# Scores and exp of the last two context blocks by halves of the queries, and other PSUM buffers and another order in the linear attention

## The chip, the cores and the metric

The kernel runs on one core of a Trainium2 chip. The metric is the device time of one execution in microseconds. The engines are TensorE (PE, matmuls; PEld, its weight loads), VectorE (DVE), ScalarE (ACT), GpSimd (POOL) and SyncE (SP, which issues the DMAs). Each works through its own instructions in order.

## What is computed

The reference is one block of a perceiver network: a cross attention of 512 queries on 8192 context tokens, a linear attention on the 512 tokens, and a feed-forward layer with quantized operands. Width is 512, with 16 heads of 32.

```python
x = x + xattn(layernorm(x), ctx, ctx, Wq, bq, Wk, bk, Wv, bv, Wo, bo)
#   q, k, v = split_heads(...); weights = softmax(q k^T / sqrt(32)); z = weights v; z Wo + bo
x = x + attn(layernorm(x), w_qkv, proj, w_out, b_out)
#   qf = elu(q proj) + 1; kf = elu(k proj) + 1       (128 features a head)
#   out = qf (kf^T v) / (qf sum(kf) + 1e-8);          out w_out + b_out
x = x + ffn(layernorm(x), W1, b1, W2, b2)
#   linear layers on operands rounded to 8 bits, gelu between them
```

## The kernel before

`network` does all of it, in stages that follow each other; a second copy of it stands under a condition at the program's end and is run only where denominators leave a range, which they do not here. Almost every instruction is passed through `in_order`, so that each engine's order is the order of the source.

**Cross attention.** The context comes in 16 blocks `b` of 512 tokens. For a block, keys `kT[b]` and values `vt[b]` are projected; for all but the last block by `blockwise` (seven products of quarter size, matmuls of 256 columns, `pm`), in the last block the keys by `project_keys` (matmuls of 512 columns, `pk`). These steps stand in a list, `queue`, and are dealt out by `ahead`, each with a cost, so that they come due evenly over the units.

A unit is (b, g, k): a block, one of 4 groups of 4 heads, and one of 4 chunks of 128 keys. The loop is `for i, u in enumerate(units)`. For a unit:

- `weights` (L788, L797): TensorE forms the scores `sc` of 128 keys, 4 heads and 512 queries, in eight matmuls of 32 rows and 64 columns, eight at a time on the array. `sc` is in PSUM, four stretches of 512 columns, one for each head. Its pool `ps_s` has one buffer. ScalarE takes exp of all of `sc` in one instruction into `ex` (four buffers).
- Then TensorE does the due projection steps (L388) and, in `weighted_sums` (L733), the product `av` of the unit before, into the pool `ps_a` of two buffers.
- `summed` (L806): VectorE adds `ex` to `acc`, from which the denominators come (`sums`, `dn`, L751; `inverse`, a reciprocal, L757).

In the last block's units `weighted_sums` stands before the due step, and `dn` is formed in between.

**Linear attention.** For each of four groups `g`: `keys(g)` and `queries(g)` project (L1007) and VectorE copies the result out of PSUM (L1012); `key_features` and `query_features` multiply with `proj` into `feat` (L1051, L1073; the pool `ps_f`, one buffer); `elu1` takes exp and relu of two halves on ScalarE (`er`, L1029) and joins them on VectorE (`f`, L1033). Between the two halves of `f` on VectorE stands what `between` does, one of the projections with its copy. `products` gives `kv` (L1085, L1091) and copies it, `turned` transposes it (`kvl`, L1101, L1103), `attended` forms the numerator and the denominator `att` (L1112) and copies the denominator (`de`, L1117), `divided` takes its reciprocal and multiplies (L1122, L1123). `out_sums` (L898) is the output projection `po`, and `out_added` (L1174, L1178) adds it to `xs` and forms statistics for the next layer norm.

PSUM here: `ps_m` (tag `pt`, two buffers), `ps_a` (tag `av`, two), `ps_f` (the size of four). After the last `feat`, `ps_f` is closed and `ps_o` (four buffers) takes its place.

**Feed-forward.** Two quantized layers with bf16 matmuls; some matmuls (`nothing`, `keep_busy`) give no result that is used and only keep TensorE occupied.

The functions that the change touches, and what calls them:

Of the kernel before, what the change touches and what calls it, by code (L numbers as in the profile page):

```python
# [8 lines left out]
F32 = mybir.dt.float32  # L9
BF16 = mybir.dt.bfloat16  # L10
AF = mybir.ActivationFunctionType
# [5 lines left out]
P = 128  # L17
# [9 lines left out]
def network(  # L27
# [24 lines left out]
    nc = tc.nc  # L52
    S, E = x.shape
    L = ctxT.shape[1]
    FF = W1T.shape[1]
    H, D = 16, 32
# [3 lines left out]
    HG = P // D  # L60
# [3 lines left out]
    SCALE = 1.0 / float(D) ** 0.5  # L64
# [12 lines left out]
    def in_order(i):  # L77

        return tc.keep_in_program_order(i)
# [6 lines left out]
    for i in range(7):  # L86
        n = 1 << i
# [190 lines left out]
    ap4 = ctx.enter_context(tc.tile_pool(name="ap4", bufs=4))  # L278
    ps_m = ctx.enter_context(tc.tile_pool(name="ps_m", bufs=2, space=PSUM))

    with ExitStack() as actx:
        aw = actx.enter_context(tc.tile_pool(name="aw", bufs=1))

        qT = aw.tile([P, NE, S], F32, name="qT")
# [11 lines left out]
        bias = aw.tile([P, NE], F32, name="bias")  # L296
# [4 lines left out]
        ct, kT, vt, tt = {}, {}, {}, {}  # L301
# [4 lines left out]
        total = first + NB  # L306
# [416 lines left out]
        ps_a = ctx.enter_context(tc.tile_pool(name="ps_a", bufs=2, space=PSUM))  # L723
        sctx = actx.enter_context(ExitStack())
        ps_s = sctx.enter_context(tc.tile_pool(name="ps_s", bufs=1, space=PSUM))
        av, late = {}, []
# [35 lines left out]
        def biased(g):  # L762
# [5 lines left out]
            else:  # L768
                in_order(nc.vector.tensor_scalar(
                    Z[:, g, :], Z[:, g, :], bv_sb[:, g : g + 1], None, ALU.add  # L770
                ))

        def weights(b, g, k):

            assert ("k", b, g, k // 2) in made
            sc = ps_s.tile([P, HG, S], F32, name="sc")
            if exact:
                for j in range(HG):
                    for h in range(2):
                        in_order(nc.tensor.matmul(  # L780
                            sc[ts(h, P // 2), j, :], lhsT=ones_h[ds(j * D, 3), ts(h, P // 2)],
                            rhs=mrow[ds(j * D, 3), g, :], start=True, stop=False,
                        ))

            for j in range(HG):
                rows = ts(j, D)
                for h in range(2):
                    in_order(nc.tensor.matmul(  # L788
                        sc[ts(h, P // 2), j, :],
                        lhsT=kT[b][rows, g, ds(k * P + h * P // 2, P // 2)],  # L790
                        rhs=qT[rows, g, :], start=not exact, stop=True,
                    ))
            ex = ap4.tile([P, HG, S], F32, name="ex")
            if exact:
                in_order(nc.scalar.activation(ex, sc, AF.Exp, scale=SCALE))
            else:
                in_order(nc.scalar.activation(  # L797
                    ex, sc, AF.Exp, bias=bias[:, g : g + 1], scale=SCALE
                ))
            return ex  # L800
# [36 lines left out]
        for i, u in enumerate(units):  # L837
            ex = weights(*u)
            if i >= last_block:
                b, g, k = u  # L840
# [48 lines left out]
        ps_o = octx.enter_context(tc.tile_pool(name="ps_o", bufs=NT, space=PSUM))  # L889
# [97 lines left out]
    with ExitStack() as lctx:  # L987
        lw = lctx.enter_context(tc.tile_pool(name="lw", bufs=1))
        lp = lctx.enter_context(tc.tile_pool(name="lp", bufs=2))
# [9 lines left out]
        eps_c = lw.tile([P, 1], F32, name="eps_c")  # L999
        nc.vector.memset(eps_c, 1e-8)  # L1000

        kT2, qT2, kf, kf_sum, qf, kvT, kvl = {}, {}, {}, {}, {}, {}, {}

        def projected(wt, g, name):
            ps = ps_m.tile([P, S], F32, name="pq2", tag="pt")
            for c in range(NE):
                in_order(nc.tensor.matmul(  # L1007
                    ps, lhsT=wt[:, c, ts(g, P)], rhs=ynT[:, c, :],
                    start=(c == 0), stop=(c == NE - 1),
                ))  # L1010
            dst = lp.tile([P, S], F32, name=name)
            in_order(nc.vector.tensor_copy(dst, ps))  # L1012
            return dst

        def keys(g):
            kT2[g] = projected(wk2_sb, g, "kT2")

        def queries(g):
            qT2[g] = projected(wq2_sb, g, "qT2")

        def elu1(ps, halves, between):


            f = ap4.tile([P, HG, S], F32, name="f", tag="ex")
            er = []
            for h in halves:
                er.append(ap2.tile([P, 2, HG // 2, S], F32, name="er", tag="vt"))
                for d, function in enumerate((AF.Exp, AF.Relu)):
                    in_order(nc.scalar.activation(  # L1029
                        er[-1][:, d].rearrange("p a n -> p (a n)"), ps[h], function  # L1030
                    ))
            for i, h in enumerate(halves):
                in_order(nc.vector.scalar_tensor_tensor(  # L1033
                    f[h], er[i][:, 0].rearrange("p a n -> p (a n)"), 1.0,
                    er[i][:, 1].rearrange("p a n -> p (a n)"), ALU.min, ALU.add,
                ))
                if i == 0:
                    between()
            return f

        by_head = [(slice(None), ts(i, HG // 2)) for i in range(2)]
        by_token = [(slice(None), slice(None), ts(i, S // 2)) for i in range(2)]
# [21 lines left out]
                kf_sum[g], half[:, :, :F], half[:, :, F:], ALU.add  # L1064
            ))

        def query_features(g, between):

            ps = ps_f.tile([P, HG, S], F32, name="feat")
            for j in range(HG):  # L1070
                rows = ts(j, D)
                for h in range(2):
                    in_order(nc.tensor.matmul(  # L1073
                        ps[ts(h, P // 2), j, :], lhsT=proj_sb[rows, g, ts(h, P // 2)],
                        rhs=qT2[g][rows, :], start=True, stop=True,
                    ))
            qf[g] = elu1(ps, by_token, between)

        def products(g):


            ps = ps_m.tile([P, 2, F], F32, name="kv", tag="pt")
            for t in range(NT):
                for j in range(HG):
                    in_order(nc.tensor.matmul(  # L1085
                        ps[ts(j, D), 0, :], lhsT=va[:, t, ds(g * P + j * D, D)],
                        rhs=kf[g][:, j, ts(t, F)],
                        start=(t == 0), stop=(t == NT - 1),
                    ))
            for j in range(HG):  # L1090
                in_order(nc.tensor.matmul(  # L1091
                    ps[ts(j, D), 1, :], lhsT=ones_c, rhs=kf_sum[g][:, j, :],
                    start=True, stop=True,
                ))
            kvT[g] = lp.tile([P, 2, F], F32, name="kvT")
            in_order(nc.scalar.copy(kvT[g], ps))

        def turned(g, copy=nc.scalar.copy):
            ps = ps_m.tile([P, 2, P], F32, name="kvl", tag="pt")
            for i in range(2):  # L1100
                in_order(nc.tensor.transpose(ps[:, i, :], kvT[g][:, i, :], ident))  # L1101
            kvl[g] = lp.tile([P, 2, P], F32, name="kvl")
            in_order(copy(kvl[g], ps))  # L1103

        def attended(g, n, pools):

            ps = []
            for i in range(2):
                pool, tag = pools
                ps.append(pool.tile([P, S], F32, name="att", tag=tag)[:, : n.size])  # L1110
                for j in range(HG):
                    in_order(nc.tensor.matmul(  # L1112
                        ps[i][ts(j, D), :], lhsT=kvl[g][:, i, ts(j, D)],
                        rhs=qf[g][:, j, n], start=True, stop=True,
                    ))
            de = lp.tile([P, S], F32, name="de")[:, : n.size]
            in_order(nc.scalar.activation(de, ps[1], AF.Identity, bias=eps_c))  # L1117
            return ps[0], de

        def divided(g, n, att):  # L1120
# [18 lines left out]
        key_features(1, lambda: queries(0))  # L1139
        products(0)  # L1140
        query_features(0, lambda: keys(2))
        turned(0), products(1)
        key_features(2, lambda: queries(1))
        turned(1)
        divided(0, every, attended(0, every, (ps_a, "av")))
        query_features(1, lambda: keys(3))
        products(2)
        key_features(3, lambda: queries(2))
        turned(2)
        divided(1, every, attended(1, every, (ps_a, "av")))  # L1150
        query_features(2, lambda: queries(3))
        products(3)


        po = [ps_m.tile([P, E], F32, name="po", tag="pt")]
# [5 lines left out]
        att = attended(2, every, (ps_a, "av"))  # L1161
# [2 lines left out]
        query_features(3, lambda: None)  # L1164

        po += [ps_m.tile([P, E], F32, name="po", tag="pt")]
        fctx.close()
        ps_o = ctx.enter_context(tc.tile_pool(name="ps_o", bufs=NT, space=PSUM))
        po += [ps_o.tile([P, E], F32, name="po2", tag="po") for _ in range(2)]

        def out_added(t):

# [8 lines left out]

        out_sums(1, [0, 1]), out_sums(2, [0, 1])
        halves = [ts(i, S // 2) for i in range(2)]
        att = attended(3, halves[0], (ps_a, "av"))
        divided(3, halves[0], att)
        out_sums(3, [0])
        att = attended(3, halves[1], (ps_o, "po"))
# [123 lines left out]
    for q in range(NF // 4):  # L1311
# [14 lines left out]
        for i in range(4):  # L1326
# [8 lines left out]
            if f < 2 or i % 2 == 1:  # L1335
                k = f if f < 2 else f // 2 + 1
# [33 lines left out]
    for i in range(len(chunks) + 1):  # L1370
        if i < len(chunks):
            f, n = chunks[i]
# [4 lines left out]
        f, n = chunks[i - 1]  # L1377
# [77 lines left out]
```

## Time and profile before

| | us |
|---|---|
| runs | 1117.04, 1117.11, 1119.11 (median 1117.11) |
| profiled execution | 1118.67, of which the span of its trace is 1116.9 |
| TensorE busy in the span | 1089.1 (98%) |
| VectorE, ScalarE, GpSimd busy | 932.2, 633.7, 177.8 |
| units of the block before the last begin | at 848.7 |
| units of the last block begin | at 902.2 |
| first output projection of the cross attention | at 957.6 |
| last matmul of the linear attention's output projection ends | at about 1059 |
| granted TensorE clock, mean | 0.995 |

A row of the profile's groups or of its timeline names the line of the kernel, the engine, the operation and the tiles (output <- inputs). In the timeline the first two columns are the start and the length in us; in square brackets stands how long the engine had been idle and which instruction ended the wait. A matmul of fp32 operands is done in two passes and shows as two records, so eight matmuls read x16. Ends of matmuls are modelled. A list of waits has: who waited <- for whom, us in total, times, the longest.

### The profile page before, as it was taken

Reading aid. Unit: us, or ns where it says so; the run is one execution under the profiler, and the core shown is the slowest. Engines: PE = TensorE matmul, PEld = TensorE weight load, DVE = VectorE, ACT = ScalarE, POOL = GpSimd, SP = SyncE. Lnnn points to the kernel's source line nnn. Section 1 sums busy time; section 2 is a strip of 40 time slices with the busy share of each in tenths; the row PEclk is TensorE's granted clock in tenths of the full one; section 3 lists DMA queues with packets and bytes.
Section 4 is the critical chain, followed back from the end, with each engine's and each line's share of the span. In section 5 each row is a group of like instructions: output and inputs, shape, how many; then the busy total and the mean of one; then the engine's idle time right before and its main releaser. Section 6 shows DMA issues by size and latency. Waiting matters only on the chain.

```text
span 1116.9 us, 31051 instructions
## 1 busy us (share of the span) xinstructions
PE 1089.1 (98%) x14331; PEld 409.7 (37%) x14336; DVE 932.2 (83%) x863; ACT 633.7 (57%) x425; POOL 177.8 (16%) x90
## 2 busy tenths in 40 slices
PE   8999999999999999999999999999999999999896
PEld 5433333333333333333333333333332321344342
DVE  3688999999888888888888888888888888756796
ACT  2155555566666666666665555555555566346253
POOL 3520303011403030403030303030300000023000
PEclk9999999999999999999999999999999999999999
DMA  7121213110302121212010101010110021130001
GB/s 264 38 79 40 96 40 96 58 59 30 95 31 68 50 76 30 75 51 68 30 58 2 40 2 40 2 39 2 40 39 2 2 77 39 38 151 2 1 1 41
DMA packets 24778, 55.56 MB, mean 50 GB/s; under 512 B 1984, under 2 KB 2496, under 8 KB 24384
## 3 DMA queue, kind: packets, MB, share of 16 engines
q1 hardware_dynamic: 24352, 52.97, 14.3%
q8 instruction: 114, 1.87, 0.7%
q10 hardware_dynamic: 288, 0.52, 0.1%
q14 instruction: 24, 0.20, 0.1%
HBM read 48.25 MB, written 5.24 MB: 48 GB/s over the span
## 4 chain that ended last, share of the span: by engine, by line
PE 88%; ACT 5%; DVE 5%; issue 1%; DMA 1%; SPq 0%; DVEq 0%; ACTq 0%
PE pm L388 35%; PE sc L788 24%; PE av L733 18%; ACT ex L797 4%; PE po L898 2%; PE pq L1007 2%; PE pq L136 1%; DVE unchanged L143 1%; PE pv L936 1%; PE pys L1356 1%; DVE de L1122 1%; ACT er L1029 1%; PE att L1112 1%; DMA ct<-in_ctxT 1%; DVE tops L631 0%
## 5 line engine op out<-in xcount | busy, mean ns | idle before, releaser
L797 ACT ACTIVATE ex<-sc,bias 128x2048 f32<-128x2048 f32 x256 | 504.3, 1970 | 358.4 <-PE sc L788 358.4
L806 DVE TENSOR_TENSOR acc<-acc,ex 128x2048 f32<-128x2048 f32 x248 | 584.8, 2358 | 73.2 <-ACT ex L797 72.9
L788 PE MATMUL sc<-qT,kT 32*64 32x512 f32 x4096 | 285.2, 613 | 6.9 <-ACT ex L797 6.7
L733 PE MATMUL av<-ex,vt 128*32 128x512 f32 x2048 | 266.9, 593 | 0.0
L383 POOL TENSOR_TENSOR tt<-ct 128x512 f32<-128x512 f32 x32 | 62.4, 1950 | 573.4 <-DMA ct<-in_ctxT 519.8
L788 PEld LDWEIGHTS sc<-qT,kT 32*64 32x64 f32 x4096 | 59.7, 129 | 221.8 <-ACT ex L797 198.0
L388 PE MATMUL pm<-w,tt 128*32 128x256 f32 x2048 | 127.0, 382 | 0.0
L388 PE MATMUL pm<-tt,w 128*32 128x256 f32 x1920 | 118.0, 382 | 0.0
L388 PE MATMUL pm<-w,ct 128*32 128x256 f32 x1536 | 96.5, 383 | 0.0
L478 DVE TENSOR_TENSOR vt<-vt,pm 128x512 f32<-128x512 f32 x112 | 75.3, 684 | 25.1 <-PE pm L388 24.1
L388 PEld LDWEIGHTS pm<-w,tt 128*32 128x32 f32 x2048 | 59.7, 109 | 86.0 <-issue 51.9
L388 PE MATMUL pm<-ct,w 128*32 128x256 f32 x1440 | 90.1, 383 | 1.2 <-DMA ct<-in_ctxT 1.2
L733 PEld LDWEIGHTS av<-ex,vt 128*32 128x32 f32 x2048 | 65.3, 110 | 55.5 <-issue 14.0
L383 POOL TENSOR_TENSOR tt<-ct,tt 128x512 f32<-128x512 f32 x32 | 85.3, 2666 | 1.3
L388 PEld LDWEIGHTS pm<-tt,w 128*32 128x32 f32 x1920 | 56.5, 109 | 77.6 <-issue 46.2
L388 PEld LDWEIGHTS pm<-w,ct 128*32 128x32 f32 x1536 | 43.3, 109 | 73.8 <-issue 47.0
L388 PEld LDWEIGHTS pm<-ct,w 128*32 128x32 f32 x1440 | 41.2, 109 | 67.2 <-issue 44.1
L478 DVE TENSOR_TENSOR kT<-kT,pm 128x512 f32<-128x512 f32 x60 | 40.8, 680 | 27.6 <-PE pm L388 27.0
L481 DVE SCALAR_TENSOR_TENSOR kT<-pm,bk_sb,kT 128x256 f32<-128x256 f32 x90 | 39.0, 474 | 2.9 <-PE pm L388 1.0
L745 DVE TENSOR_TENSOR Z<-Z,av 128x512 f32<-128x512 f32 x60 | 40.6, 677 | 0.0
L1029 ACT ACTIVATE er<-feat 128x1024 f32<-128x1024 f32 x32 | 30.2, 1029 | 9.7 <-PE feat L1051 7.4
L1033 DVE SCALAR_TENSOR_TENSOR f<-er 128x1024 f32<-128x1024 f32 x16 | 19.9, 1248 | 13.6 <-ACT er L1029 13.6
(181 smaller groups left out, 585.7 us busy)
## 6 DMA issues: line engine op xcount, KB each, us to landing
ct<-in_ctxT SPq DMA_DIRECT2D x15, 1024.0 KB, 5.3
wraw<-in_W1T SPq DMA_DIRECT2D x16, 512.0 KB, 3.8
wraw<-in_W2T SPq DMA_DIRECT2D x16, 512.0 KB, 3.8
wd<-wquant SPq DMA_DIRECT2D x16, 256.0 KB, 2.4
w_q<-wd SPq DMA_DIRECT2D x2, 2048.0 KB, 10.6
w<-in_w_qkv SPq DMA_DIRECT2D x3, 1024.0 KB, 5.1
w<-in_Wk SPq DMA_DIRECT2D x2, 512.0 KB, 6.5
ct<-in_ctxT SPq DMA_DIRECT2D x2, 512.0 KB, 7.5
```

What stands on the lines that cost most here:

```text
L383: in_order(nc.gpsimd.tensor_tensor(tt[b][:, i], x, y, ALU.subtract))
L388: in_order(nc.tensor.matmul(ps[ts(j, D)], lhsT=lhsT[:, ts(j, D)], rhs=rhs, start=start, stop=stop))
L478: in_order(nc.vector.tensor_tensor(dst, src, ps, ALU.add))
L481: in_order(nc.vector.scalar_tensor_tensor(dst[:, m, :], ps[:, m, :], bk_sb[:, 2 * i + m : 2 * i + m + 1], src[:, m, :], ALU.add, ALU.add,))
L733: in_order(nc.tensor.matmul(av[g][ts(j, D), :], lhsT=vt[b][:, k, ds(g * P + j * D, D)], rhs=ex[:, j, :], start=(k == 0), stop=(k == NC - 1),))
L745: in_order(nc.vector.tensor_tensor(Z[:, g, :], Z[:, g, :], ps, ALU.add))
L788: in_order(nc.tensor.matmul(sc[ts(h, P // 2), j, :], lhsT=kT[b][rows, g, ds(k * P + h * P // 2, P // 2)], rhs=qT[rows, g, :], start=not ex ...
L797: in_order(nc.scalar.activation(ex, sc, AF.Exp, bias=bias[:, g : g + 1], scale=SCALE))
L806: in_order(nc.vector.tensor_tensor(acc[:, g], acc[:, g], ex, ALU.add))
L898: in_order(nc.tensor.matmul(po, lhsT=lhsT[:, c, ts(t, P)], rhs=w[:, c, :], start=(c == 0), stop=(c == NE - 1),))
L1007: in_order(nc.tensor.matmul(ps, lhsT=wt[:, c, ts(g, P)], rhs=ynT[:, c, :], start=(c == 0), stop=(c == NE - 1),))
L1029: in_order(nc.scalar.activation(er[-1][:, d].rearrange("p a n -> p (a n)"), ps[h], function))
```

## The change

There are two edits in one.

1. In the last two blocks (`b >= total - 2`, 32 of the 256 units) `weights` forms the scores of queries 0 to 255, takes their exp, and then does the same for queries 256 to 511. One `sc` tile is kept for all of these units.
2. In the linear attention: `turned(0)` takes its buffer from `ps_a`; `attended` forms the denominator before the numerator and copies it at once; in `query_features(1)` and `(2)` the projection and its copy stand ahead of both halves of `f`; the output tiles of tokens 256 to 511 come from `ps_a`, and the first half of group 3's `att` from `ps_o`.

GpSimd's and SyncE's instructions and their order are as before. ScalarE has 32 more instructions, TensorE 256 more matmuls of half the columns in place of whole ones.

```diff
+        halved = {}
+
         def weights(b, g, k):
 
             assert ("k", b, g, k // 2) in made
+            if not exact and b >= total - 2:
+                if "sc" not in halved:
+                    halved["sc"] = ps_s.tile([P, HG, S], F32, name="sc")
+                sc = halved["sc"]
+                ex = ap4.tile([P, HG, S], F32, name="ex")
+                for q in range(2):
+                    n = ts(q, S // 2)
+                    for j in range(HG):
+                        rows = ts(j, D)
+                        for h in range(2):
+                            in_order(nc.tensor.matmul(
+                                sc[ts(h, P // 2), j, n],
+                                lhsT=kT[b][rows, g, ds(k * P + h * P // 2, P // 2)],
+                                rhs=qT[rows, g, n], start=True, stop=True,
+                            ))
+                    in_order(nc.scalar.activation(
+                        ex[:, :, n], sc[:, :, n], AF.Exp, bias=bias[:, g : g + 1], scale=SCALE
+                    ))
+                return ex
             sc = ps_s.tile([P, HG, S], F32, name="sc")
...
-        def elu1(ps, halves, between):
+        def elu1(ps, halves, between, at=1):
...
             for i, h in enumerate(halves):
+                if i == at:
+                    between()
                 in_order(nc.vector.scalar_tensor_tensor(
                     f[h], er[i][:, 0].rearrange("p a n -> p (a n)"), 1.0,
                     er[i][:, 1].rearrange("p a n -> p (a n)"), ALU.min, ALU.add,
                 ))
-                if i == 0:
-                    between()
...
-        def query_features(g, between):
+        def query_features(g, between, at=1):
...
-            qf[g] = elu1(ps, by_token, between)
+            qf[g] = elu1(ps, by_token, between, at)
...
-        def turned(g, copy=nc.scalar.copy):
-            ps = ps_m.tile([P, 2, P], F32, name="kvl", tag="pt")
+        def turned(g, copy=nc.scalar.copy, pool=ps_m, tag="pt"):
+            ps = pool.tile([P, 2, P], F32, name="kvl", tag=tag)
...
         def attended(g, n, pools):
 
-            ps = []
-            for i in range(2):
+            ps = {}
+            for i in (1, 0):
                 pool, tag = pools
-                ps.append(pool.tile([P, S], F32, name="att", tag=tag)[:, : n.size])
+                ps[i] = pool.tile([P, S], F32, name="att", tag=tag)[:, : n.size]
...
-            de = lp.tile([P, S], F32, name="de")[:, : n.size]
-            in_order(nc.scalar.activation(de, ps[1], AF.Identity, bias=eps_c))
+                if i == 1:
+                    de = lp.tile([P, S], F32, name="de")[:, : n.size]
+                    in_order(nc.scalar.activation(de, ps[1], AF.Identity, bias=eps_c))
             return ps[0], de
...
-        turned(0), products(1)
+        turned(0, pool=ps_a, tag="av"), products(1)
...
-        query_features(1, lambda: keys(3))
+        query_features(1, lambda: keys(3), 0)
...
-        query_features(2, lambda: queries(3))
+        query_features(2, lambda: queries(3), 0)
...
         po += [ps_m.tile([P, E], F32, name="po", tag="pt")]
+        po += [ps_a.tile([P, E], F32, name="po2", tag="av") for _ in range(2)]
         fctx.close()
         ps_o = ctx.enter_context(tc.tile_pool(name="ps_o", bufs=NT, space=PSUM))
-        po += [ps_o.tile([P, E], F32, name="po2", tag="po") for _ in range(2)]
...
-        att = attended(3, halves[0], (ps_a, "av"))
+        att = attended(3, halves[0], (ps_o, "po"))
```

## The prediction

> **What bounds the kernel now.** I read the page's busy table and chain first, then the groups of the score loop, then the timeline and the waits from 848 to 958 us (the last two blocks), and last the clock by windows.
>
> ```profile
> PE 1089.1 (98%) x14331; PEld 409.7 (37%) x14336; DVE 932.2 (83%) x863; ACT 633.7 (57%) x425; POOL 177.8 (16%) x90
> PE 88%; ACT 5%; DVE 5%; issue 1%; DMA 1%; SPq 0%; DVEq 0%; ACTq 0%
> L797 ACT ACTIVATE ex<-sc,bias 128x2048 f32<-128x2048 f32 x256 | 504.3, 1970 | 358.4 <-PE sc L788 358.4
> ```
>
> TensorE sets the time; ScalarE idles 358 us in front of the exp. The exception is the last two blocks. There the timeline shows a unit that TensorE cannot start on time:
>
> ```profile
> 853.72 1.97 ACT L797 ACTIVATE ex<-sc,bias 128x2048 f32<-128x2048 f32 x1 [1.80 <-PE sc L788]
> 855.74 1.12 PE L788 MATMUL sc<-qT,kT 32*64 32x512 f32 x16 [0.27 <-ACT ex L797]
> 856.78 1.92 PE L388 MATMUL pk<-ct,w 128*32 128x512 f32 x16
> 856.96 1.97 ACT L797 ACTIVATE ex<-sc,bias 128x2048 f32<-128x2048 f32 x1 [1.27 <-PE sc L788]
> ```
>
> Read four prices here. Exp's end to the next scores: 853.72 + 1.97 = 855.69, then 855.74, so 0.05. Scores' start to exp's start: 856.96 - 855.74 = 1.22. Exp: 1.97. Scores' start to the next thing on TensorE: 856.78 - 855.74 = 1.04. The loop scores, exp, scores takes 1.22 + 1.97 + 0.05 = 3.24 us, whatever TensorE has to do. All waits of this kind, from 848 to 958 us:
>
> ```profile
> PE sc L788 <- ACT ex L797: 6.4, 20, 1.1
> ```
>
> **Units of the last two blocks before.** Each matmul of the source is two records. A unit of TensorE alone is scores, av, and steps: four matmuls of 256 columns are 0.43 us, four of 512 columns (pk, dn) 0.86. Starts of scores at 777.71, 781.48 and 784.81 give 3.77 us with four steps of 0.43 and 3.33 with three, so a unit not held by exp lasts 2.05 + 0.43 c, c counting steps of 0.43. Read off the timeline, the 16 units from 848.73 have c = 4 2 4 2 2 2 3 2 3 2 3 2 3 2 3 3, and the 16 from 902.22 have 2 2 2 2 2 4 2 2 2 4 2 0 2 4 2 2: together 78. That is 32 x 2.047 + 78 x 0.43 = 99.0 us. From 848.73 to the last dn at 955.77 the trace has 107.0. So 8.0 us is lost to exp; nothing else is there to be won in this stage.
>
> **What the change makes of it.** Scores and exp of a unit are cut into query halves 0 and 1, in one tile `sc` that is kept for all 32 units. TensorE's order is half 0, half 1, steps, av, next half 0. In the built program the first matmul of half 1 waits for ScalarE's count of the exp of half 0 of the same unit, in all 32 units; half 0 of the next unit waits for the exp of half 1. Both halves lie in the same four 512-column stretches of `sc` (one for each head), and the program lets neither engine into them while the other is there. So the halves do not overlap: exp of half 0 now stands in the middle of TensorE's in-order queue, with half 1, the steps and av behind it.
>
> Here a page speaks against the change: the Trainium skill, PSUM — Partial Sum Buffer, "PSUM bank collisions raise a hardware error", says that TensorE writing and ScalarE reading one bank and quadrant at once is an error even in disjoint columns, and that one should synchronise by bank; 512 fp32 values are one bank there. By it the wait cannot be dropped while the cut goes through the banks; no run here shows a collision.
>
> Prices of the halves; the trace has no such shape.
> - Scores of 64 x 256. Rows on both sides: 16 records of 512 columns take 1.22 to their reader, 64 records of 128 columns (key features, 987.04 to 988.28) take 1.24. Both stream 512 columns through their eight tiles, as a set of av does through its four, and that takes 0.86 (its weight loads come at 853.99 and 854.42, four in 0.43, eight to a set). So about 0.37 is fixed, and a half is 0.43 + 0.37 = 0.80 to exp and 0.43 + 0.18 = 0.61 to the next TensorE work. Ends: 0.61 (half of 1.22) and 1.22 (no saving). I take 0.80, as both rows give that fixed part.
> - Exp of 128 x 1024. Same engine without a bias: 1.03 (L1029). With a bias, but out of SBUF: 1.24 (L228). From 256 columns 0.475 (L1117), 512 0.68 (L405) and 2048 1.97, all with a bias out of PSUM, the slope is 0.83 ns a column: 1.12. I take 1.12.
>
> A unit now: half 0 to exp 0.80, exp 1.12, hand-over 0.05, half 1 0.61, then 2.05 - 1.04 = 1.01 for av and switches, and the steps: 3.58 + 0.43 c. That is 1.53 more than TensorE alone needs. The exp of half 1 ends 0.80 + 1.12 + 0.05 + 0.80 + 1.12 = 3.89 after the unit's start, which is hidden behind TensorE for c of 1 and more; the one unit with c = 0 waits 0.35.
> Sum: 32 x 3.58 + 33.5 + 0.35 = 148.4 against 107.0, **+41.4 us**. The 8.0 lost before is inside: it is won, and 49 is paid. VectorE's acc (2.29 a unit) and the ring of four `ex` have more room than before; the Z and kT copies on ScalarE (0.7) fall into its idle time.
>
> **Linear attention**, by the waits between 957 and 1062 us that the edits touch:
>
> ```profile
> PE kv L1085 <- ACT kvl L1103: 0.5, 1, 0.5
> PE feat L1051 <- DVE kT L1012: 0.9, 1, 0.9
> PE po L898 <- DVE qT L1012: 0.8, 1, 0.8
> PE po L898 <- ACT er L1029: 2.0, 1, 2.0
> ```
>
> - `turned(0)` in ps_a: kv of group 1 no longer takes the buffer of kvl. -0.5; kf_sum on POOL (ends 1006.77) is next, after kv's first part, so it hides.
> - Denominator first, copies of keys(3) and queries(3) ahead of f: the copies now need only their projection and the divide. The reciprocal (3.35) starts 0.9 earlier and is out of the way. kT is ready at 1020.2, before products end at 1020.6. -0.9 and -0.8. Of f the end stays (1022.6), since the same work is done in another order; its reader comes at 1026.6 or 0.9 earlier.
> - po2 in ps_a: out_sums(2) follows out_sums(1) at once: -2.0, and its four records take 1.73 instead of 3.38 (half clock, below): -1.65. Late next is f of group 3: its first half ends at 1045.07, or 1042.9 with the 2.2 already won, and TensorE is free at 41.7, so att(3) waits 1.2. Net -2.5.
> Together **-4.7**; ends: 0, if the later chain of VectorE (out_added to y_ext) takes it back, and -6.
>
> **Sum.** 41.4 - 4.7 = +36.7 on the profiled execution's 1118.67 us (span 1116.9, 1.8 around it): 1155.4. The median, 1117.11, is 1.6 lower and gives 1153.8. I say **1154.5**.
>
> **Rivals.**
> 1. *Faster: half 1 runs beside the exp of half 0.* TensorE then alone sets a unit: -8.0 - 4.7, plus 32 x 0.03 for more instructions (the 128-column features leave TensorE after 1.13, the 512-column ones after 1.04, for four times the records): 1107 us. For it: TensorE has nothing else to wait for. Against: the wait in the program. It would decide once half 1 came less than 0.40 us late in a unit instead of 1.53 (12.7/32). 0.04.
> 2. *Serial, and the clock falls.* TensorE now idles 1.3 us in each unit. The windows of TensorE (columns: length, busy, granted clock) show where it fell before:
>
> ```profile
> 1041.30:1044.70 3.40, 1.38 (x4) 1.00 0.00 0
> 1044.70:1048.10 3.40, 3.40 (x8) 0.51 0.00 0
> 1061.80:1065.20 3.40, 1.84 (x10) 1.00 0.00 0
> 1065.20:1068.60 3.40, 3.16 (x13) 0.51 0.00 0
> 1089.10:1092.50 3.40, 1.95 (x9) 1.00 0.00 0
> 1092.50:1095.90 3.40, 2.01 (x10) 1.00 0.00 0
> ```
>
> After 1.38 and 1.84 busy of 3.4 the next 3.4 us run at half clock, after 1.95 and 2.01 not. A window with one whole gap has 3.4 - 1.3 = 2.1: above, by little. If some fall under, each costs about 1.3 us (some 2.6 us of matmuls in it at half speed); six to twenty of the 43 windows in 148 us: +8 to +26, so 1162 to 1181. 0.11. [...]
> 3. *Serial, but halves cost exactly half* (0.61 and 0.99): 32 x (0.19 + 0.13) = 10 less, 1144. Against: every row has a fixed part. 0.05.
> The forecast itself: 0.80.
>
> **How the numbers follow.** What a measurement of this kernel can tell from no change is about 0.2%, 2 us. All serial cases (0.96) are slower, rival 1 is faster; 0.01 I leave for same, out of the serial cases. For the range: exp between 1.03 and 1.24 is -3 to +4; scores towards rival 3, -6; linear attention +5 to -1; the lower dips of the clock +8. It is 1146 to 1168; outside lie rival 1, most of rival 3 and the upper half of rival 2.
>
> **What would show it.** Right: two exps of about 1.12 for each unit, the scores of half 1 with some 1.3 us of TensorE idle put down to the exp, 32 times; scores starts 4.4 apart where c is 2, 4.9 where it is 3; waits of scores for exp some 40 to 50 us in the last two blocks; linear attention starting some 41 us later and ending 36 to 37 later; the dip after 1041 gone. Wrong: half 1 starting while the first exp runs (rival 1), clock under 1.00 between 849 and 1000 (rival 2), or an exp half near 0.99 (rival 3).

## The result and the profile after

The changed kernel takes **1155.86 us** (median of 4 runs, 1154.86 to 1156.63) against 1118.03 us of the kernel before on the same chip (4 runs, 1117.04 to 1119.11): a ratio of 1.0335, 95% interval 1.0322 to 1.0348. Its profiled execution took 1155.12 us, with a span of 1153.2 us.

The page of the kernel after: busy times, the chain by engine, and the groups of the halves (operation | busy us, mean ns of one | idle time ahead of them and what ended it).

```profile
PE 1093.1 (95%) x14848; PEld 416.3 (36%) x14848; DVE 931.4 (81%) x863; ACT 641.9 (56%) x457; POOL 176.8 (15%) x90
PE 90%; DVE 4%; ACT 4%; issue 1%; DMA 1%; SPq 0%; ACTq 0%; DVEq 0%
L795 ACT ACTIVATE ex<-sc,bias 128x1024 f32<-128x1024 f32 x64 | 71.3, 1113 | 70.6 <-PE sc L790 70.6
L790 PE MATMUL sc<-qT,kT 32*64 32x256 f32 x1024 | 44.1, 400 | 41.3 <-ACT ex L795 41.3
```

TensorE's busy time is nearly the same (1093.1 against 1089.1), its share of the span falls from 98% to 95%. What is new is the idle time in the last line: TensorE stands still for 41.3 us in front of a score matmul, and an exp ends that. The waits between 848 and 1000 us (total, times, longest) tell how often:

```profile
PE sc L790 <- ACT ex L795: 41.3, 33, 1.3
ACT ex L795 <- PE sc L790: 70.6, 61, 2.2
```

Before, the first of these was 6.4 us in 20 waits. It is now 33 times 1.25: once in each of the 32 units for half 1, and once more for the half 0 of the unit with c = 0. The timeline of a unit with c = 4 (start, duration, engine, operation):

```profile
858.88 0.69 PE L790 MATMUL sc<-qT,kT 32*64 32x256 f32 x16
859.67 1.11 ACT L795 ACTIVATE ex<-sc,bias 128x1024 f32<-128x1024 f32 x1 [1.36 <-PE sc L790]
...
860.84 0.69 PE L790 MATMUL sc<-qT,kT 32*64 32x256 f32 x16 [1.27 <-ACT ex L795]
...
861.46 1.92 PE L388 MATMUL pk<-ct,w 128*32 128x512 f32 x16
861.63 1.11 ACT L795 ACTIVATE ex<-sc,bias 128x1024 f32<-128x1024 f32 x1 [0.85 <-PE sc L790]
...
864.17 0.47 PE L790 MATMUL sc<-qT,kT 32*64 32x256 f32 x8
```

Half 0 starts at 858.88, its exp 0.79 later, that ends at 860.78, and half 1 starts at 860.84. In between TensorE has the due projections and av to do, which wait for nothing, but in its order they stand behind half 1. The two exps never have a matmul of `sc` beside them. The unit lasts 5.29 us; the one ahead of it (854.44 to 858.88, c = 2) 4.44.

The two blocks run from 849.13 to 997.69 us, 148.6 us against 107.0, and the linear attention starts 41.9 us later than before. It then makes some of it up. Each row is the start of an instruction (or of a group of equal ones) in the two timelines.

| instruction | before | after | shift | gained since the row above |
|---|---|---|---|---|
| last dn of the cross attention | 955.77 | 997.69 | +41.92 | |
| kv of group 1 | 1006.66 | 1048.02 | +41.36 | 0.56 |
| feat of keys(3) | 1021.61 | 1062.00 | +40.39 | 0.97 |
| first po | 1035.23 | 1074.74 | +39.51 | 0.88 |
| att of group 3, first half | 1047.80 | 1084.67 | +36.87 | 2.64 |
| out_added of the first tile | 1054.01 | 1090.32 | +36.31 | 0.56 |

Behind that row the shift stays: `pe`, ten us on, starts at 1063.92 before and 1100.23 after, 36.31 us later too.

### The profile page after: what moved, and what is told of

Its sections match the earlier page's. It is cut to its first block, busy times and chain, and to the rows that moved or that the text cites. A ratio compares the mean times of both kernels' runs of the same rounds, so it can differ in the third digit from the quotient of the medians.

```text
span 1153.2 us, 32116 instructions
## 1 busy us (share of the span) xinstructions
PE 1093.1 (95%) x14848; PEld 416.3 (36%) x14848; DVE 931.4 (81%) x863; ACT 641.9 (56%) x457; POOL 176.8 (15%) x90
## 4 chain that ended last, share of the span: by engine, by line
PE 90%; DVE 4%; ACT 4%; issue 1%; DMA 1%; SPq 0%; ACTq 0%; DVEq 0%
PE pm L388 35%; PE sc L811 20%; PE av L733 19%; PE sc L790 4%; ACT ex L795 3%; PE pq L1030 3%; PE po L921 1%; PE pk L388 1%; PE pq L136 1%; DVE unchanged L143 1%; PE pv L959 1%; PE pys L1380 1%; PE dn L751 1%; DMA ct<-in_ctxT 1%; DVE de L1146 1%
## 5 line engine op out<-in xcount | busy, mean ns | idle before, releaser
L820 ACT ACTIVATE ex<-sc,bias 128x2048 f32<-128x2048 f32 x224 | 441.1, 1969 | 318.5 <-PE sc L811 318.5
L811 PE MATMUL sc<-qT,kT 32*64 32x512 f32 x3584 | 249.5, 613 | 0.5 <-ACT ex L820 0.3
L383 POOL TENSOR_TENSOR tt<-ct 128x512 f32<-128x512 f32 x32 | 57.6, 1800 | 574.4 <-DMA ct<-in_ctxT 432.0
L811 PEld LDWEIGHTS sc<-qT,kT 32*64 32x64 f32 x3584 | 52.1, 129 | 187.2 <-ACT ex L820 163.4
L795 ACT ACTIVATE ex<-sc,bias 128x1024 f32<-128x1024 f32 x64 | 71.3, 1113 | 70.6 <-PE sc L790 70.6
L383 POOL TENSOR_TENSOR tt<-ct,tt 128x512 f32<-128x512 f32 x32 | 89.2, 2786 | 1.3
L790 PE MATMUL sc<-qT,kT 32*64 32x256 f32 x1024 | 44.1, 400 | 41.3 <-ACT ex L795 41.3
L790 PEld LDWEIGHTS sc<-qT,kT 32*64 32x64 f32 x1024 | 15.0, 129 | 82.7 <-ACT ex L795 71.0
```

The lines of the kernel that those rows point to most:

```text
L383: in_order(nc.gpsimd.tensor_tensor(tt[b][:, i], x, y, ALU.subtract))
L790: in_order(nc.tensor.matmul(sc[ts(h, P // 2), j, n], lhsT=kT[b][rows, g, ds(k * P + h * P // 2, P // 2)], rhs=qT[rows, g, n], start=True, ...
L795: in_order(nc.scalar.activation(ex[:, :, n], sc[:, :, n], AF.Exp, bias=bias[:, g : g + 1], scale=SCALE))
L811: in_order(nc.tensor.matmul(sc[ts(h, P // 2), j, :], lhsT=kT[b][rows, g, ds(k * P + h * P // 2, P // 2)], rhs=qT[rows, g, :], start=not ex ...
L820: in_order(nc.scalar.activation(ex, sc, AF.Exp, bias=bias[:, g : g + 1], scale=SCALE))
```

## The experiments

All were timed against the kernel before on their own chip (1118.5 to 1119.3 us there), so ratios compare best.

**1. Edit 1 alone** (halves, with the linear attention of before):

```diff
-        turned(0, pool=ps_a, tag="av"), products(1)
+        turned(0), products(1)
...
-        query_features(1, lambda: keys(3), 0)
+        query_features(1, lambda: keys(3))
...
```

> The halves of edit 1 alone, with the linear attention of before. If the loss is the halves' and the linear attention wins what its waits said: 41.4 us above before (ratio 1.037), 3 to 4 us above the changed kernel, and the last two blocks last 148.5 us from their first scores to the last dn, as in the changed kernel. Rival: the two edits share or disturb each other (the clock, phases of the windows); then it lies at or below the changed kernel's time.

Measured: 1162.31 us, ratio 1.038 (1.0359 to 1.0401). The waits of scores for exp are again 41.3 us in 33 waits.

**2. Edit 2 alone** (linear attention as changed, `weights` as before):

```diff
-            if not exact and b >= total - 2:
-                if "sc" not in halved:
...
-                return ex
             sc = ps_s.tile([P, HG, S], F32, name="sc")
```

> Edit 2 alone. From the trace of the changed kernel its linear attention takes 5.6 us less: 1112.4 us, ratio 0.995. If the gain came only with the delayed start (another phase of the clock's windows), it is smaller, down to nothing: ratio 0.998 to 1.0.

Measured: 1113.97 us, ratio 0.9953 (0.9938 to 0.9969), 5.3 us faster. The two edits add up: +3.80% and -0.47% give +3.33%, against +3.35% for both. The loss is all in the halves.

**3. The scores cut in halves, the exp whole.** This keeps the smaller matmuls and takes away the wait between them. It is built on edit 1 alone, so the linear attention is that of before:

```diff
-                    in_order(nc.scalar.activation(
-                        ex[:, :, n], sc[:, :, n], AF.Exp, bias=bias[:, g : g + 1], scale=SCALE
-                    ))
+                in_order(nc.scalar.activation(
+                    ex, sc, AF.Exp, bias=bias[:, g : g + 1], scale=SCALE
+                ))
```

> Only the score matmuls of the last two blocks are cut into query halves (16 matmuls of 256 columns for a unit in place of 8 of 512); exp is one instruction for the whole unit; linear attention as before. If the wait between the halves is the cost: nothing to wait for, 0 to 3 us above before (0.03 to 0.09 a unit). If the smaller matmuls themselves cost (a fixed part for each half, 0.19 to 0.37 us a unit): 6 to 12 us above before.

Measured: 1118.80 us, ratio 0.9998 (0.9986 to 1.0011). The page's group of the score matmuls:

```profile
L790 PE MATMUL sc<-qT,kT 32*64 32x256 f32 x1024 | 35.9, 387 | 6.4 <-ACT ex L795 6.4
```

The timeline of the first unit of the last two blocks in the same kernel:

```profile
848.74 1.12 PE L790 MATMUL sc<-qT,kT 32*64 32x256 f32 x32
...
849.79 1.93 PE L388 MATMUL pm<-w,ct 128*32 128x256 f32 x32
849.97 1.97 ACT L795 ACTIVATE ex<-sc,bias 128x2048 f32<-128x2048 f32 x1 [1.37 <-PE sc L790]
```

The same 1024 records as in the changed kernel, with 6.4 us of idle time ahead of them instead of 41.3, as before the change. From the scores to the next matmul it is 1.05 us (whole: 1.04), to exp 1.23 (whole: 1.22). Cutting the matmuls costs 0.01 us a unit; the exp between them is what costs.

**4. The due work between the halves.** In the changed kernel, half 1 is put behind the unit's due projections, in the last block behind its weighted sums:

```diff
-                for q in range(2):
+                def half(q):
...
+                half(0)
+                later.append(lambda: half(1))
                 return ex
...
+                while later:
+                    later.pop(0)()
```

> The changed kernel, with half 1 of the scores behind the unit's due projections (in the last block behind its weighted sums) instead of straight behind half 0. Theory (only the wait costs): half 1 then finds its exp ended, and a unit takes the two chains of 0.80 + 1.11 + 0.05 us that cannot overlap, 3.92 us at the least, and for c = 3 about 4.1 and c = 4 about 4.5 us, against 4.44 at c = 2 and 5.29 at c = 4 in the changed kernel. Over 32 units 128 to 130 us instead of 148.6 us: 1135 to 1138 us, still slower than before. Rival (the halves' smaller instructions are what costs): no change from 1155 us.

Measured: 1136.84 us, ratio 1.0162 (1.0144 to 1.0180). One unit with c = 2, from its half 0 (885.42) over its half 1 (887.39) to the half 0 of the next (889.35):

```profile
885.42 0.69 PE L792 MATMUL sc<-qT,kT 32*64 32x256 f32 x16 [0.28 <-ACT ex L797]
886.05 1.07 PE L388 MATMUL pm<-w,tt 128*32 128x256 f32 x16
...
887.39 0.69 PE L792 MATMUL sc<-qT,kT 32*64 32x256 f32 x16 [0.27 <-ACT ex L797]
888.01 1.06 PE L733 MATMUL av<-ex,vt 128*32 128x512 f32 x8
...
889.35 0.69 PE L792 MATMUL sc<-qT,kT 32*64 32x256 f32 x16 [0.28 <-ACT ex L797]
```

The gap of 1.27 us is now filled by projections and 0.28 is left; the unit lasts 3.93 us, twice the chain of 0.80 + 1.11 + 0.05. The same instructions in another order give back 19 of the 38 us. The chain itself stays: 32 units of 3.92 us are 125 us, against 107.0 for the two blocks before, as long as the tile lets only one of the two engines in at a time.

**5. Halves in four blocks instead of two:**

```diff
-            if not exact and b >= total - 2:
+            if not exact and b >= total - 4:
```

> The changed kernel with the halves in the last four blocks instead of the last two. Theory: in the two blocks added TensorE was busy throughout (100.0 of 100.0 us from 600 to 700 us), so each of the 32 more units pays the whole +1.53 us over TensorE's own time: +49 us on 1155.9, 1204 to 1206 us. Rival (the loop only pays what its own hand-over of 3.24 us falls short of): a unit there pays less, as its TensorE work is longer and hides part of the second exp: +25 to +40 us.

Measured: 1204.58 us, ratio 1.0763 (1.0745 to 1.0782): 48.7 us more than the changed kernel, for 32 more units 1.52 each (by the ratios, as the two were timed on different chips, 47.9 and 1.50). The window of TensorE from 740 to 840 us (length, busy, granted clock) in the kernel before:

```profile
740.00:840.00 100.00, 100.00 (x1468) 1.00 0.10 32
```

The same window with halves in four blocks:

```profile
740.00:840.00 100.00, 74.52 (x1336) 1.00 0.08 23
```

TensorE goes from full to three quarters. Where TensorE had nothing to wait for before, all of the +1.53 over its own time is paid, as in the last two blocks.

**6. Whole scores, exp by pairs of heads, two tiles.** Scores of heads 0, 1 and of heads 2, 3 get a tile each, so that one can be filled while the other is read. The linear attention is as changed, here and below.

```diff
+                    for p in range(2):
+                        halved[p] = pool.tile([P, HG // 2, S], F32, name=f"sc{p}")
...
+                            halved[j // 2][ts(h, P // 2), j % 2, :],
...
+                for p in range(2):
+                    in_order(nc.scalar.activation(
+                        ex[:, ts(p, HG // 2), :], halved[p], AF.Exp,
```

> Whole scores, but exp by pairs of heads, each pair's scores in a tile of its own of two of the four 512-column stretches, so that scores of heads 0 and 1 wait only for their own exp; linear attention as changed. If the wait through the shared tile is the cost, two exps a unit do no harm: a unit with c = 2 should take about 3.05 us (2.90 for TensorE alone; 3.24 before), the two blocks about 102 to 103 us in place of 107, in all some 10 us below before: 1108, ratio 0.991. If cutting exp in two costs by itself (2.13 of ScalarE in place of 1.97 for each of 32 units), it is not below the linear attention alone: 1112 to 1118.

Measured: 1111.93 us, ratio 0.9936 (0.9920 to 0.9951). Faster than before, but short of the 1108 us expected.

**7. The same, with each pair's exp right behind its own matmuls in the program:**

```diff
+                for p in range(2):
+                    for j in range(2 * p, 2 * p + 2):
...
+                                halved[p][ts(h, P // 2), j % 2, :],
...
+                    in_order(nc.scalar.activation(
+                        ex[:, ts(p, HG // 2), :], halved[p], AF.Exp,
```

> As the run with two tiles by pairs of heads, but each pair's exp stands right behind its own four matmuls in the program, so that the first exp need not wait for all eight: 0.80 us instead of the 1.16 us from the start of the scores seen there. The first exp then ends at 0.80 + 1.11 = 1.91 us and the second at about 2.97 us, and the next block's scores of heads 2 and 3 may start at 3.02 us, 0.43 us behind the start of their block: a unit of at least 2.59 us, below TensorE's own 2.91 us at c = 2. Theory (the wait comes from the shared tile): the two blocks take TensorE's own 99.0 us and about 1.5 us for the units with c = 0 and 1, 100.5 us against 107.0 before: -6.5, with -5.6 from the linear attention 1106.6 us, a ratio of 0.989. Rival (two exp calls of 1.11 us cost the loop more than one of 1.97 us, whatever the tiles): not below 1111.9 us, as with the exps behind all matmuls.

Measured: 1111.92 us, ratio 0.9939 (0.9926 to 0.9952): nothing won, so the expected 0.80 to the first exp was wrong. Two units of it in the timeline:

```profile
902.45 1.11 PE L791 MATMUL sc<-qT,kT 32*64 32x512 f32 x16
...
903.60 2.12 ACT L796 ACTIVATE ex<-sc,bias 128x1024 f32<-128x1024 f32 x2 [1.21 <-PE sc L791]
...
905.35 1.52 PE L791 MATMUL sc<-qT,kT 32*64 32x512 f32 x16
905.77 0.21 PEld L791 LDWEIGHTS sc<-qT,kT 32*64 32x64 f32 x8 [0.22 <-ACT ex L796]
906.50 2.12 ACT L796 ACTIVATE ex<-sc,bias 128x1024 f32<-128x1024 f32 x2 [0.78 <-PE sc L791]
```

The first exp starts 1.15 us after the scores, as behind all four heads (1.16 in experiment 6): the pairs fill different rows of the array at the same time, so two heads take as long as four. The second exp ends at 905.72, and only then (905.77) may heads 2, 3 of the next unit follow its heads 0, 1, which started at 905.35. These scores take 1.52 us instead of 1.11, and units last 2.90 and 3.30 us in turn.

**8. The same order in one tile.** Against experiment 7 only the tile differs:

```diff
-                    for p in range(2):
-                        halved[p] = pool.tile([P, HG // 2, S], F32, name=f"sc{p}")
+                    halved["sc"] = ps_s.tile([P, HG, S], F32, name="sc")
...
-                                halved[p][ts(h, P // 2), j % 2, :],
+                                sc[ts(h, P // 2), j, :],
...
-                        ex[:, ts(p, HG // 2), :], halved[p], AF.Exp,
+                        ex[:, ts(p, HG // 2), :], sc[:, ts(p, HG // 2), :], AF.Exp,
```

> The same order as the kernel with two tiles by pairs of heads, alternated, but in the one tile of four stretches. Each stretch is written and read by one pair of heads only, so no stretch is shared between what runs side by side. Theory A (the wait covers the whole tile): the chain is that of the changed kernel, 2 x (0.80 + 1.11 + 0.05) less what the last hand-over hides, 3.58 + 0.43c us a unit, and the time stays at 1155 to 1157 us. Theory B (the wait covers only stretches that are truly read and written): as with two tiles, about 1107 us.

Measured: 1220.06 us, ratio 1.0910 (1.0889 to 1.0930), 108 us more than with two tiles. Theory B falls. Theory A holds for the wait, but the time is 64 us above its 1155 to 1157 us. The timeline of one unit, from its second part to the next unit's first:

```profile
899.94 1.09 PE L789 MATMUL sc<-qT,kT 32*64 32x512 f32 x8 [1.24 <-ACT ex L794]
...
900.96 2.56 PE L388 MATMUL pm<-w,tt 128*32 128x256 f32 x24
901.10 1.11 ACT L794 ACTIVATE ex<-sc,bias 128x1024 f32<-128x1024 f32 x1 [1.21 <-PE sc L789]
...
904.94 0.21 PEld L789 LDWEIGHTS sc<-qT,kT 32*64 32x64 f32 x8 [1.45 <-issue]
904.94 1.09 PE L789 MATMUL sc<-qT,kT 32*64 32x512 f32 x8
```

Two heads alone (x8) hold TensorE for 1.02 us to the next matmul, where four (x16) take 1.05. That adds some 0.4 us to each of a unit's two parts. The first takes 1.16 to its exp, 1.11 for the exp and 0.05 for the hand-over, 2.32 us; with the second and the rest a unit is 2.32 + 2.05 + 0.43c = 4.37 + 0.43c instead of 3.58 + 0.43c, which gives 32 x 0.79 = 25 us on the changed kernel's 1155.9, or 1181 us. The rest, 39 us, is put down to the clock, and experiment 9 tests that. The pm group of 24 records takes 2.56 us here and 1.50 in experiment 4. Windows of TensorE in experiment 8 (length, busy, granted clock):

```profile
855.80:859.20 3.40, 2.17 (x20) 1.00 0.00 0
859.20:862.60 3.40, 2.17 (x24) 1.00 0.00 0
862.60:866.00 3.40, 3.40 (x24) 0.66 0.00 0
```

**9. All four heads in both parts.** The gaps of experiment 8 were no longer than those of the changed kernel (1.24 against 1.27 us). What differed was how much of the array the scores fill. So here each part computes all four heads; the same scores are written twice, and nothing else is moved:

```diff
-                    for j in range(2 * p, 2 * p + 2):
+                    for j in range(HG):
```

> As the kernel with pairs of heads in one tile, alternated, but each of the two parts computes the scores of all four heads instead of two, so that the same scores are written twice. A part of two heads took as long there as four heads took before (1.02 against 1.05 us to the next matmul), so order, waits and gaps (1.24 us of idle TensorE in every unit) stay as they were; only the share of the array that the score matmuls fill goes from a half to the whole. Theory (the clock fell there because half-filled score matmuls count as half): the granted clock stays at 1.00, a unit takes 2.32 + 2.05 + 0.43c us, 173 us for the 32 units against 148.6 us in the changed kernel, and the time is about 1181 us. Rival (the gaps made the clock fall): the clock is again 0.7 to 0.9 in the two blocks and the time stays at 1215 to 1222 us.

Measured: 1181.96 us, ratio 1.0562 (1.0534 to 1.0591), 38 us less than experiment 8 with twice the score matmuls. The two parts of a unit in its timeline:

```profile
904.15 1.11 PE L789 MATMUL sc<-qT,kT 32*64 32x512 f32 x16
906.54 1.12 PE L789 MATMUL sc<-qT,kT 32*64 32x512 f32 x16 [1.27 <-ACT ex L794]
```

Its window from 900 to 950 us (length, then busy time and instructions of PE, PEld, DVE, ACT and POOL, granted clock):

```profile
900.00:950.00 50.00, 37.90 (x512) 10.58 (x512) 26.45 (x18) 20.59 (x19) 0.00 (x0) 1.00 0.14 43
```

In experiment 8, three such stretches:

```profile
850.00:900.00 50.00, 38.89 (x333) 9.88 (x334) 21.82 (x13) 20.09 (x19) 0.00 (x0) 0.90 0.00 1
900.00:950.00 50.00, 41.35 (x332) 11.56 (x336) 20.22 (x14) 16.48 (x15) 0.00 (x0) 0.79 0.07 22
950.00:1000.00 50.00, 41.36 (x252) 7.54 (x241) 22.43 (x13) 16.50 (x16) 0.00 (x0) 0.77 0.06 22
```

TensorE's busy time there contains matmuls that the low clock made longer. So the short windows ahead of the first fall compare better. Those shown for experiment 8 have 2.17 us busy each; the same windows here, with the clock kept:

```profile
855.80:859.20 3.40, 2.13 (x36) 1.00 0.00 0
859.20:862.60 3.40, 2.13 (x36) 1.00 0.00 0
862.60:866.00 3.40, 3.40 (x40) 1.00 0.00 0
```

With the gaps kept and the array filled the clock stays at 1.00, though TensorE is busy for no more of the time than where it fell.

## Why the prediction was right

It said 1154.5 us, and 1155.86 was measured (1155.4 on the basis of the profiled execution, where 1155.12 was measured).

- **The wait was read from the program, and it is there.** Half 1 stands behind the exp of half 0 in every unit, with 1.27 us of idle time ("some 1.3" was said). Experiment 4 fills the gap and wins 19 us; experiment 3 takes the exp from between the halves and all of the loss goes with it.
- **Prices of the halves.** Scores to exp 0.79 (0.80 said), to the next matmul 0.62 (0.61), exp 1.11 (1.12), hand-over 0.06 (0.05). So a half does not cost half: the fixed 0.37 us of the scores is paid twice, and so is what exp has beyond its columns (2 x 1.11 against 1.97). Rival 3, halves at exactly half the price, fell with this.
- **The unit.** 3.58 + 0.43c: 4.44 us was both said and measured for c = 2; for c = 0 (975.15 to 979.07) 3.92 measured, 3.58 + 0.35 = 3.93 said. The two blocks took 148.6 us, 148.4 said.
- **The reason given for the wait was too narrow.** The prediction put it down to the four stretches that both halves share. Experiment 8 has no shared stretch, each pair of heads has its own two, and the wait is as long. Experiment 7 differs from it by the tile alone and does not have it. So in the built program the two engines wait for each other by the whole tile.
- **The linear attention was under-sized by 0.9 us**: -5.6 in the trace, -4.7 said, inside the ends given (0 and -6). 0.56, 0.97, 0.88 and 2.64 stand against 0.5, 0.9, 0.8 and 2.5, the new wait of att for f is 1.05 (1.2 said). Left out was the last row of the table, 0.56: in group 3 too the denominator is formed first, and its copy starts 0.76 us after att's start (1084.67 to 1085.43) instead of 1.32 (1047.80 to 1049.12). Some 0.17 of it is the clock, which was 0.50 at the start of that att before: from there to the next matmul it was 1.17 us before and 1.00 after. Experiment 2 measured 5.3.
- **Rival 2, the clock, did not come**: it was 1.00 in all windows from 840 to 1000 us, with 2.07 to 2.12 of 3.40 us busy in the sparsest, and 1.79 in one. The dip after 1041 us of before is gone, as said; that at 1065 us is gone as well, which was not said. Experiment 8 shows that the rival was no fancy: with pairs of heads, and gaps no longer, the clock did fall and cost 38 us.
- **Rival 1, overlap,** needed what experiments 6 and 7 built by other means, a second tile. Even there the two blocks do not come down to TensorE's own 99 us. In experiment 7 they take 105.3 us (848.91 to the start of the last dn at 954.16): the tile of heads 2, 3 is free 3.3 us after the unit's start, and a unit of TensorE alone with c = 2 is 2.9.
- **Halves of the queries in two tiles were not tried**, so it stays open what they would take. With the layout of `sc` kept, both halves of a head lie in one stretch of 512 fp32 values, one bank by the Trainium skill, PSUM — Partial Sum Buffer, whose section "PSUM bank collisions raise a hardware error" warns of two engines in one bank at once; no run here shows such a collision, and none has a layout that keeps the halves apart.

The fastest kernels of the study are those with two tiles by pairs of heads, 1111.9 us, 0.6% below before. Most of this is the changed linear attention. Experiments 2 and 6 ran on one chip, and their ranges do not meet (1113.45 to 1115.57 and 1111.77 to 1112.77): the two tiles add 2.0 us. The traces say the same, 105.3 us for the two blocks against 107.0.

## What to carry to other kernels

Cutting a producer and a consumer into halves overlaps nothing as long as both halves live in one tile that the program guards as a whole: before counting the gain, look up in the built program which instruction the second half waits for, and what is queued behind it on its engine. Price a half by its fixed part plus its columns, never by half of the whole, and for matmuls that share the array ask first whether half of them takes any less time. If the wait has to stay, put work that is ready between the halves.

## What the runs showed of the hardware

- **The granted clock fell with half of the array's tiles idle in the scores, though the gaps were the same.** Experiments 8 and 9 have one order, and gaps of 1.24 and 1.27 us. With four of the array's eight tiles of 32 x 64 at work in the scores the clock went to 0.77 to 0.90 in stretches of 50 us, with all eight it stayed at 1.00. Neither the busy time tells them apart (2.17 of 3.4 us in the two windows ahead of the first fall, 2.07 to 2.13 in the sparsest of experiment 9) nor the bare number of matmuls: before, neighbouring windows of 9 and 10 matmuls (1.95 and 2.01 us busy) kept the clock, and in experiment 8 windows of 20 and 24 lost it. At which filling it falls no run here tells. The Trainium skill, TensorE: Matmul & The Clock Gate, "Part 1: The HAM clock gate", has the half clock follow an idle window of about 3.4 us, and reports one kernel in which frequent short idle times between groups of matmuls made the clock go up and down. Experiment 8 had no idle stretch above 1.24 us where the clock first fell, and in experiment 9 gaps as long left it at 1.00.
- **Eight small matmuls of 32 rows and 64 columns take nearly as long as four**: 1.05 against 1.02 us to the next matmul. Leaving out half of the heads saves 0.03 us, as they run side by side.
- **Smaller matmuls cost next to nothing by themselves here**: 16 of 256 columns took 1.05 us to the next matmul where eight of 512 took 1.04.
